# Two Mamba layers: du times B for two slots in succession, then both scans, and y's transposes ahead of B's spread

## The chip, the cores and the metric

The kernel runs on one core of a Trainium2 chip. The core has five engines that run side by side, each through its own list of instructions in order: TensorE (PE, matrix products; PEld is its weight load), VectorE (DVE), ScalarE (ACT), GpSimd (POOL) and SyncE (SP, which issues the transfers). They wait for one another through semaphores. The metric is the device time of one execution in microseconds (us): a median over several executions, and beside it one execution that was profiled.

## The reference

The network has four residual layers on an image of 4 batches, 256 channels, 64 x 64 pixels: two attention layers (L0, L1), then a Mamba layer over 512 inner channels (L2), then a Mamba layer over four groups of 64 channels with an MLP (L3). The change touches the state recurrence of L2 and L3. For each batch, each inner channel d and each of 16 states n:

```
delta = softplus(dt @ dt_proj_w + dt_proj_b)
A = -exp(A_log)
def step(h, (d_t, u_t, B_t, C_t)):
    h   = exp(d_t * A) * h + (d_t * u_t) * B_t
    y_t = sum over n of h * C_t
h0 = 0;  ys = scan(step, h0, over 4096 tokens)
y = ys + u * D
y = y * silu(z)
out = y @ out_proj_w
```

So each (channel, state) pair has a linear recurrence over the tokens, B and C are shared by all the channels of a token, and y is summed over the 16 states.

## The kernel before

**Tiles, blocks and slots.** The tokens of a batch (4096) are cut in 4 chunks of NC = 1024, and the inner channels in 4 groups of 128 (in L3, the four channel groups have 128 inner channels each). One group of one chunk is a block, with 128 channels on the partitions and 1024 tokens along the free dimension. There are 16 blocks for a batch and a layer, and each has DS = 16 slots, one for each state n. `scan_blocks` goes through the 256 slots of a batch and a layer in one loop, by hand: the order in which the calls stand is the order on each engine. It runs 8 times (two layers, four batches), so there are 2048 slots. In between lie the attention layers and the layers' beginnings and ends, which the change does not touch.

**What one slot i does, by engine.**

- `load_c` (SP, L925) brings C's row to all partitions (`cb`); three slots ahead.
- `spread` (PE, L949) makes B's row on all partitions by two products of 512 columns into a PSUM tile `pb`. The PSUM pool `psb` has two such tiles, so the tile of slot i+2 is that of slot i, and spread(i+2) waits until the scan of slot i has read it.
- In the slots named by `apart` (n = 0, 5, 10 in L2, 0, 4, 8 in L3) B comes by a transfer into `bb` instead (L931), GpSimd multiplies it with du (`product`, L935), and the decay exp(delta A) goes into the PSUM tile (`dap`, ACT, L961) in the place of B.
- In all other slots VectorE multiplies B with du in place in PSUM (L1019), and the decay is an SBUF tile `da` (ACT, L961, four buffers, three slots ahead).
- The scan (DVE, L1025) makes h of 1024 tokens. The last slot of a run is done in two halves.
- GpSimd multiplies h with C (`hc`, L1031, three buffers).
- `turn` (PE, L977) transposes hc in eight pieces of 128 columns and adds them up in a PSUM tile y over the 16 states. It is done one slot late: slot i's body turns slot i-1.
- `keep` (ACT, L966) puts the last column of h away as the next chunk's state.

**What else stands in a slot's body.** `blk["bg"]` holds steps of other work (projections, convolutions, norms and MLP of neighbouring blocks) by slot number; `end` finishes the block before (fin_ps on PE at L998 and L1002, then a product on VectorE at L991). In a body the order is: product and scan on DVE; GpSimd's product(i+2) and hc; ACT's decay(i+3) and keep; the loads; the steps of `bg` and `end`; spread(i+2); steps named n + 0.5; turn(i-1); `dap` of slot i+2. So on TensorE each body is: other work, spread of slot i+2, transposes of slot i-1.

**PSUM.** Two `pb` tiles of two banks, one y tile of two banks, and two tiles `mm` of one bank for everything else.

Of the kernel before, what the change touches and what calls it, by code (L numbers as in the profile page):

```python
# [12 lines left out]
ALU = mybir.AluOpType  # L13
# [31 lines left out]
class Net:  # L45
# [858 lines left out]

    def scan_blocks(self, blocks, loop, psum, psb, psy, apart, ends, first, last=None):
        nc = self.nc
        slots = [(blk, n) for blk in blocks for n in range(DS)]
        halves = [slice(s, s + NT) for s in range(0, NC, NT)]  # L910
        pb, da, cb, h, hc = {}, {}, {}, {}, {}
        n_slot, n_f32 = len(slots), 2


        def is_apart(i):
            return 0 < i < n_slot and slots[i][1] in apart

        def pieces(i):
            return halves if i == n_slot - 1 else [slice(0, NC)]

        def load_c(i):
            if i < len(slots):
                blk, n = slots[i]
                cb[i] = loop.tile([P, NC], F32, tag="cb", name="cb", bufs=4)
                nc.sync.dma_start(cb[i], blk["cd"][1, n].partition_broadcast(P))  # L925

        def load_b(i):
            if is_apart(i):
                blk, n = slots[i]
                pb[i] = loop.tile([P, NC], F32, tag="bb", name="bb", bufs=1)  # L930
                nc.sync.dma_start(pb[i], blk["cd"][0, n].partition_broadcast(P))  # L931

        def product(i):
            if is_apart(i):
                nc.gpsimd.tensor_tensor(pb[i], slots[i][0]["du"], pb[i], ALU.mult)  # L935

        def spread(i):
            if i < len(slots) and not is_apart(i):
                blk, n = slots[i]
                pb[i] = psb.tile([P, NC], F32, tag="pb", name="pb")  # L940
                for ss in halves:
                    if i < n_f32:
                        nc.tensor.matmul(
                            pb[i][:, ss],
                            self.ident[64:P, 64 + n : 65 + n].to_broadcast([64, P]),
                            blk["bct"][64:P, ss], start=True, stop=True,
                        )
                        continue
                    nc.tensor.matmul(  # L949
                        pb[i][:, ss], self.pick[:, n : n + 1].to_broadcast([P, P]),  # L950
                        blk["parts"][:, ss], start=True, stop=True,
                    )

        def decay(i, in_psum=False):
            if i < len(slots) and is_apart(i) == in_psum:
                blk, n = slots[i]
                if in_psum:
                    da[i] = psb.tile([P, NC], F32, tag="pb", name="dap")
                else:
                    da[i] = loop.tile([P, NC], F32, tag="da", name="da", bufs=4)  # L960
                nc.scalar.activation(da[i], blk["delta"], AF.Exp, scale=blk["a"](n))  # L961

        def keep(i):
            if i >= 0 and not slots[i][0]["last"]:
                blk, n = slots[i]
                nc.scalar.activation(blk["state"](n), h[i][:, NC - 1 : NC], AF.Copy)  # L966


        def turn(i):
            if i >= 0:  # L970
                blk, n = slots[i]
                if n == 0:
                    blk["y"] = psy.tile([P, NC], F32, tag="y", name="y")
                t = hc.pop(i)
                for j in range(NC // P):
                    ss = slice(j * P, j * P + P)
                    nc.tensor.matmul(  # L977
                        blk["y"][:, ss], t[:, ss], self.ident, is_transpose=True,
                        start=(n == 0 and ss.start % NT == 0),
                        stop=(n == DS - 1 and ss.stop % NT == 0),  # L980
                    )

        def end(blk, n):
            if n == ends[0]:
                for ss in halves:
                    nc.scalar.activation(blk["du"][:, ss], blk["y"][:, ss], AF.Copy)
            for j, (ss, first) in enumerate(zip(halves, ends[1:])):
                if n == first + 1:  # L990
                    nc.vector.tensor_tensor(  # L991
                        blk["zs"][:, ss], blk["out", j], blk["zs"][:, ss], ALU.mult
                    )
                if n == first:
                    blk["out", j] = ps = psum.tile([P, NT], F32, tag="mm", name="fin_ps")
                    for i in range(NT // P):
                        t = slice(ss.start + i * P, ss.start + i * P + P)
                        nc.tensor.matmul(  # L998
                            ps[:, i * P : (i + 1) * P], blk["du"][:, t], self.ident,
                            is_transpose=True, start=(i == 0), stop=False,  # L1000
                        )
                    nc.tensor.matmul(ps, blk["diag_d"], blk["u"][:, ss], start=False, stop=True)  # L1002

        for i in range(3):
            load_c(i)
        for i in range(4):
            load_b(i)
        for i in range(2):
            spread(i)
        for i in range(3):  # L1010
            decay(i)
            for f in first[i]:
                f()
        for i in range(2):
            decay(i, True)
            product(i)
        for i, (blk, n) in enumerate(slots):
            if not is_apart(i):
                nc.vector.tensor_tensor(pb[i], blk["du"], pb[i], ALU.mult)  # L1019
            h[i] = loop.tile([P, NC], F32, tag="h", name="h", bufs=3)  # L1020
            for ss in pieces(i):
                state = 0.0 if blk["first"] else blk["state"](n)
                if ss.start:
                    state = h[i][:, ss.start - 1 : ss.start]
                nc.vector.tensor_tensor_scan(  # L1025
                    h[i][:, ss], da[i][:, ss], pb[i][:, ss], state, ALU.mult, ALU.add
                )
            product(i + 2)
            hc[i] = loop.tile([P, NC], F32, tag="hc", name="hc", bufs=3)
            for ss in pieces(i):  # L1030
                nc.gpsimd.tensor_tensor(hc[i][:, ss], h[i][:, ss], cb[i][:, ss], ALU.mult)  # L1031
            decay(i + 3)
            keep(i - 1)
            load_c(i + 3)
            load_b(i + 4)
            if i >= DS and n != ends[0]:
                end(slots[i - DS][0], n)
            for step in blk["bg"].get(n, ()):
                step()
            if i >= DS and n == ends[0]:  # L1040
                end(slots[i - DS][0], n)
            spread(i + 2)
            for step in blk["bg"].get(n + 0.5, ()):
                step()
            turn(i - 1)
            decay(i + 2, True)
            for d in (pb, da, cb):
                del d[i]
        if last:
            last()  # L1050
        turn(n_slot - 1)
        for n in range(ends[2] + 2):
            end(blocks[-1], n)
# [168 lines left out]
    def mamba_layer(self, x, bridge, pe_dram, w_in, w_cw, w_x, w_dt, w_out, v_dram):  # L1222
        tc, nc = self.tc, self.nc
        ND = 4
        with ExitStack() as ctx:
            wp = ctx.enter_context(tc.tile_pool(name="m2_w", bufs=1, reuse_waits="tile"))
            work = ctx.enter_context(tc.tile_pool(name="m2_a", bufs=2, reuse_waits="tile"))
            loop = ctx.enter_context(tc.tile_pool(name="m2_b", bufs=2, reuse_waits="tile"))
            dram = ctx.enter_context(tc.tile_pool(name="m2_d", bufs=2, space=DRAM))
            psum = ctx.enter_context(tc.tile_pool(name="m2_p", bufs=2, space=PSUM))  # L1230
            psb = ctx.enter_context(tc.tile_pool(name="m2_q", bufs=2, space=PSUM))
            psy = ctx.enter_context(tc.tile_pool(name="m2_y", bufs=1, space=PSUM))
# [33 lines left out]
            chunks = [dict(u=[None] * ND, blocks=[]) for _ in range(n_chunk)]  # L1266
            for k in range(n_chunk):
                for d in range(ND):
# [3 lines left out]
                        first=(k == 0), last=(k == n_chunk - 1), bg={},  # L1272
# [262 lines left out]
            first = slice(0, NT), slice(NT, NC)  # L1535
# [3 lines left out]
            def center():  # L1539
# [12 lines left out]
                    )  # L1552

            self.scan_blocks(
                [blk for c in chunks for blk in c["blocks"]], loop, psum, psb, psy, (0, 5, 10),
                (1, 2, 4), (xs0[4:6], (), xs0[6:]), center,
            )
            late_square, late_sums, late_squares, finish = late_stats
# [45 lines left out]
    def grouped_mamba_layer(self, x, bridge, begun, ws_dram, outc_dram, v_dram, out_b, load):  # L1604
        tc, nc = self.tc, self.nc
        w_in, w_cw, w_x, w_dt, w_out, w_f1, w_f2 = ws_dram
        with ExitStack() as ctx:
            wp = ctx.enter_context(tc.tile_pool(name="m3_w", bufs=1, reuse_waits="tile"))
            work = ctx.enter_context(tc.tile_pool(name="m3_a", bufs=2, reuse_waits="tile"))
            loop = ctx.enter_context(tc.tile_pool(name="m3_b", bufs=2, reuse_waits="tile"))  # L1610
# [31 lines left out]
            chunks = [dict(blocks=[]) for _ in range(n_chunk)]  # L1642
# [324 lines left out]
            for i, (k, c) in enumerate(pairs):  # L1967
# [51 lines left out]
                    put(odd, (9, 11, 10, 11, 12), delta(nk, 2 * ncol))  # L2019
                    put(odd, (13, 14), [in_z(nk, ncol, s) for s in range(2)])  # L2020
            self.scan_blocks(
                [blk for c in chunks for blk in c["blocks"]], loop, psum, psb, psy, (0, 4, 8),
                (1, 2, 2), (xs0[2:4], (), xs0[4:]),
            )

# [161 lines left out]
```

## Time and profile before

| | |
|---|---|
| Median of 3 runs | 11817.76 us (11803.92 to 11832.72) |
| The profiled execution | 11811.95 us, its span 11810.1 us |
| Span of the eight runs of `scan_blocks` (windows, rounded) | 7563 us together |
| VectorE / TensorE / GpSimd / ScalarE busy in these | 7006.5 / 6128.5 / 6600.8 / 4689.8 us |
| Mean granted TensorE clock | 0.936 of full speed |

The profile gives each engine's busy time, groups of instructions (line, engine, output and inputs, shape, count, busy time, mean duration, idle time just before them and what ended it), the waits between engines and a timeline. A TensorE duration is modelled and overlaps its neighbours: two products of 0.59 us each start 0.43 us apart.

### The profile page before, as it was taken

The numbers are of one execution on the slowest core, as the hardware profiler recorded it, in microseconds if no ns is written. First come the engines' busy times: TensorE is split into PE (matmuls) and PEld (weight loads), VectorE is DVE, ScalarE is ACT, GpSimd is POOL, SyncE is SP. The second block draws the span as 40 slices with busy tenths as digits, with TensorE's granted clock in tenths as the row PEclk, the third lists the DMA queues.
The fourth block names the chain that finished last, engine by engine and source line by source line (L and its number), as shares of the span: only waits on it lengthen the run. The fifth ranks groups of instructions, "written<-read, shape, count | busy, mean of one in ns | idle before, by whom it ended". The sixth has DMA issues, their size and how long they took to land. (4 is left out here: it accounts for less than half of the span.)

```text
span 11810.1 us, 191909 instructions
## 1 busy us (share of the span) xinstructions
PE 9965.7 (84%) x70632; PEld 5738.0 (49%) x71104; DVE 9804.7 (83%) x8342; ACT 7028.2 (60%) x13152; POOL 8773.6 (74%) x6070
## 2 busy tenths in 40 slices
PE   8998887777999888777799988877779998887777
PEld 4564554444456455444455645444435564544444
DVE  6678998998767799899876779989987678998998
ACT  4565555776456555577645655557764565555776
POOL 4666886898456688789745668868975566886897
PEclk9999998998999999899999989989999999998998
DMA  3354554454335455455433545545543354554554
GB/s 97 106 141 140 172 175 143 170 183 158 94 99 144 139 172 176 144 169 183 162 88 98 144 140 172 177 143 168 182 162 90 98 143 142 172 175 143 168 175 153
DMA packets 682507, 1742.11 MB, mean 148 GB/s; under 512 B 88896, under 2 KB 194896, under 8 KB 681312
## 3 DMA queue, kind: packets, MB, share of 16 engines
q1 hardware_dynamic: 676448, 1721.41, 45.3%
q8 instruction: 563, 9.22, 0.3%
q10 hardware_dynamic: 5120, 8.39, 0.3%
q14 instruction: 376, 3.08, 0.1%
HBM read 1601.52 MB, written 94.39 MB: 144 GB/s over the span
## 5 line engine op out<-in xcount | busy, mean ns | idle before, releaser
L1031 POOL TENSOR_TENSOR hc<-h,cb 128x1024 f32<-128x1024 f32 x2056 | 4808.6, 2350 | 794.5 <-DVE h L1025 345.2
L1025 DVE TENSOR_TENSOR_SCAN h<-da,m_state,pb 128x1024 f32<-128x1024 f32 x1248 | 2920.4, 2340 | 163.0 <-DVE pb L1019 1.9
L977 PE MATMUL y<-ident,hc 128*128 128x128 f32 x16384 | 2352.7, 291 | 446.4 <-POOL hc L1031 346.1
L977 PEld LDWEIGHTS y<-ident,hc 128*128 128x128 f32 x16384 | 2051.5, 151 | 1126.1 <-POOL hc L1031 573.0
L1019 DVE TENSOR_TENSOR pb<-du,pb 128x1024 f32<-128x1024 f32 x1672 | 2025.0, 1211 | 126.4 <-PE pb L949 103.9
L961 ACT ACTIVATE da<-delta,m_v 128x1024 f32<-128x1024 f32 x1672 | 1899.2, 1141 | 135.3 <-DVE h L1025 118.4
L949 PE MATMUL pb<-m_parts,pick 128*128 128x512 bf16 x2840 | 976.1, 414 | 842.0 <-DVE h L1025 772.6
L603 POOL TENSOR_SCALAR pr<-pr,sm,zero 128x256 f32<-128x256 f32 x2048 | 1107.2, 556 | 385.5 <-DVE sm L600 381.0
L588 ACT ACTIVATE pr<-sc,mn 128x256 f32<-128x256 f32 x2048 | 954.9, 478 | 515.7 <-DVE sm L600 399.1
L949 PEld LDWEIGHTS <-pick 128*128 128x128 bf16 x3312 | 263.7, 101 | 1788.1 <-DVE h L1025 976.7
L577 DVE TENSOR_REDUCE mn<-sc 128x4 f32<-128x1024 f32 x512 | 630.1, 1232 | 542.9 <-PE sc L565 542.8
L1025 DVE TENSOR_TENSOR_SCAN h<-da,pb 128x1024 f32<-128x1024 f32 x424 | 969.5, 2287 | 55.2 <-DVE pb L1019 1.0
L935 POOL TENSOR_TENSOR bb<-du,bb 128x1024 f32<-128x1024 f32 x376 | 888.3, 2363 | 118.1 <-DMA bb<-m_cd 110.1
L1025 DVE TENSOR_TENSOR_SCAN h<-dap,m_state,bb 128x1024 f32<-128x1024 f32 x288 | 672.3, 2334 | 66.7 <-ACT dap L961 48.7
L252 PE MATMUL conv_ps<-att_y,att_wb 128*128 128x512 f32 x1536 | 682.5, 594 | 0.0
L616 PE MATMUL pt_ps<-ident,pr 128*128 128x128 f32 x4096 | 637.9, 292 | 37.8 <-POOL pr L603 16.8
L565 PE MATMUL sc<-kv,q_swap 32*64 32x128 f32 x8192 | 594.5, 283 | 26.6 <-DMA kv<-kv_dram 9.8
L961 ACT ACTIVATE dap<-delta,m_v 128x1024 f32<-128x1024 f32 x376 | 419.7, 1116 | 314.6 <-DVE h L1025 239.3
L565 PE MATMUL sc<-kv,att_y 32*64 32x128 f32 x7168 | 577.1, 282 | 28.7 <-DMA kv<-kv_dram 22.9
L616 PEld LDWEIGHTS pt_ps<-ident,pr 128*128 128x128 f32 x4096 | 459.3, 146 | 165.6 <-POOL pr L603 108.4
L290 DVE SCALAR_TENSOR_TENSOR lp<-vimg,att_v,lp 128x512 f32<-128x512 f32 x672 | 507.7, 756 | 30.4 <-DVE lp L290 0.5
L565 PEld LDWEIGHTS sc<-kv,att_y 32*64 32x64 f32 x7168 | 428.1, 136 | 161.3 <-ACT pr L588 70.5
(303 smaller groups left out, 17818.2 us busy)
## 6 DMA issues: line engine op xcount, KB each, us to landing
cb<-m_cd SPq DMA_DIRECT2D x2048, 512.0 KB, 3.9
kv<-kv_dram SPq DMA_DIRECT2D x1984, 128.0 KB, 2.8
bb<-m_cd SPq DMA_DIRECT2D x376, 512.0 KB, 5.0
kv_dram<-kst SPq DMA_DIRECT2D x128, 256.0 KB, 3.4
kv_dram<-vn SPq DMA_DIRECT2D x128, 256.0 KB, 4.2
q_swap<-att_y SPq DMA_DIRECT2D x96, 256.0 KB, 4.3
m_pe<-in_pe_dram SPq DMA_DIRECT2D x32, 512.0 KB
out_dram<-yo SPq DMA_DIRECT2D x64, 256.0 KB, 2.0
```

The costliest lines, as they stand in the source:

```text
L252: nc.tensor.matmul(ps, w[:, k, w0 + m * P : w0 + (m + 1) * P], src[:, k], start=(k == 0), stop=(k == 1),)
L565: nc.tensor.matmul(sc[h][b * 64 : b * 64 + 64, r, w, m, :], (own(sj, m) if r == b else swap[sj % 2][:, m])[rows, 2 * a + w], kv[i, w][rows ...
L588: nc.scalar.activation(t[:, g].rearrange("p j r t -> p r j t"), sc[h][:, :, g // 2, g % 2, :].rearrange("p r (j t) -> p r j t", j=2), AF.E ...
L603: nc.gpsimd.tensor_scalar(t[:, g], t[:, g], s[:, g : g + 1], self.zero, ALU.mult, ALU.add)
L616: nc.tensor.transpose(pt[h][j][:, g, :], t[:, g, j].rearrange("p r t -> p (r t)"), self.ident,)
L935: nc.gpsimd.tensor_tensor(pb[i], slots[i][0]["du"], pb[i], ALU.mult)
L949: nc.tensor.matmul(pb[i][:, ss], self.pick[:, n : n + 1].to_broadcast([P, P]), blk["parts"][:, ss], start=True, stop=True,)
L961: nc.scalar.activation(da[i], blk["delta"], AF.Exp, scale=blk["a"](n))
L977: nc.tensor.matmul(blk["y"][:, ss], t[:, ss], self.ident, is_transpose=True, start=(n == 0 and ss.start % NT == 0), stop=(n == DS - 1 and ...
L1019: nc.vector.tensor_tensor(pb[i], blk["du"], pb[i], ALU.mult)
L1025: nc.vector.tensor_tensor_scan(h[i][:, ss], da[i][:, ss], pb[i][:, ss], state, ALU.mult, ALU.add)
L1031: nc.gpsimd.tensor_tensor(hc[i][:, ss], h[i][:, ss], cb[i][:, ss], ALU.mult)
```

## The change

The loop of `scan_blocks` gets a further list of state numbers, `twos`: (2, 4, 7, 9, 12, 14) in L2, (2, 6, 10, 12, 14) in L3. Slot i is the first of two when slot i+1 has its number in that list, i is above 4 and i is not the last. In that case:

- du times B of slots i and i+1 are both issued on VectorE, and then the scan of i, what the body of i has for VectorE, and the scan of i+1;
- in the body of i, turn(i-1) stands ahead of spread(i+2) instead of behind it.

No instruction is added or removed.

```
+    def scan_blocks(self, blocks, loop, psum, psb, psy, apart, twos, ends, first, last=None):
...
+        def with_next(i):
+            return 4 < i < n_slot - 1 and slots[i + 1][1] in twos
+
+        def times_du(i):
+            if not is_apart(i):
+                nc.vector.tensor_tensor(pb[i], slots[i][0]["du"], pb[i], ALU.mult)
...
         for i, (blk, n) in enumerate(slots):
-            if not is_apart(i):
-                nc.vector.tensor_tensor(pb[i], blk["du"], pb[i], ALU.mult)
+            if not (i and with_next(i - 1)):
+                times_du(i)
+            if with_next(i):
+                times_du(i + 1)
             h[i] = loop.tile([P, NC], F32, tag="h", name="h", bufs=3)
...
+            if with_next(i):
+                turn(i - 1)
             spread(i + 2)
             for step in blk["bg"].get(n + 0.5, ()):
                 step()
-            turn(i - 1)
+            if not with_next(i):
+                turn(i - 1)
             decay(i + 2, True)
...
-                [blk for c in chunks for blk in c["blocks"]], loop, psum, psb, psy, (0, 5, 10),
+                [blk for c in chunks for blk in c["blocks"]], loop, psum, psb, psy, (0, 5, 10), (2, 4, 7, 9, 12, 14),
...
-                [blk for c in chunks for blk in c["blocks"]], loop, psum, psb, psy, (0, 4, 8),
+                [blk for c in chunks for blk in c["blocks"]], loop, psum, psb, psy, (0, 4, 8), (2, 6, 10, 12, 14),
```

More of the change, by code (lines that the diff above doesn't have):

```diff
@@ L896, in col_stats @@
         )
-    def scan_blocks(self, blocks, loop, psum, psb, psy, apart, ends, first, last=None):
+    def scan_blocks(self, blocks, loop, psum, psb, psy, apart, twos, ends, first, last=None):
         nc = self.nc
```

## The prediction

> **What bounds the kernel now.** I read first the page's groups by line, then the busy time of the eight scan stretches, then the timeline of a quiet and of a crowded piece of them. Some rows of the groups (line, engine, operation, count | busy, mean ns | idle before, releaser):
>
> ```profile
> L1031 POOL TENSOR_TENSOR hc<-h,cb 128x1024 f32<-128x1024 f32 x2056 | 4808.6, 2350 | 794.5 <-DVE h L1025 345.2
> L1025 DVE TENSOR_TENSOR_SCAN h<-da,m_state,pb 128x1024 f32<-128x1024 f32 x1248 | 2920.4, 2340 | 163.0 <-DVE pb L1019 1.9
> L1019 DVE TENSOR_TENSOR pb<-du,pb 128x1024 f32<-128x1024 f32 x1672 | 2025.0, 1211 | 126.4 <-PE pb L949 103.9
> L949 PE MATMUL pb<-m_parts,pick 128*128 128x512 bf16 x2840 | 976.1, 414 | 842.0 <-DVE h L1025 772.6
> ```
>
> VectorE hardly waits before products and scans, while TensorE's spread (L949) waits for the scan. The busy time by stretch, for the fourth stretch (L3) and the sum of all eight (us, then PE, PEld, DVE, ACT, POOL):
>
> ```profile
> 4916.00:5867.00 951.00, 729.59 (x3427) 402.87 (x3487) 873.25 (x531) 662.20 (x959) 852.33 (x388) 0.91 0.52 175
> sum 7563.00, PE 6128.47 PEld 3476.03 DVE 7006.50 ACT 4689.80 POOL 6600.81; mean PE 766.06 PEld 434.50 DVE 875.81 ACT 586.23 POOL 825.10
> ```
>
> VectorE is busy for 7006 of 7563 us; it is the bound here, with GpSimd (6601) and TensorE (6128) not far below. Now VectorE's rows in a quiet piece:
>
> ```profile
> 10735.66 1.21 DVE L1019 TENSOR_TENSOR pb<-du,pb 128x1024 f32<-128x1024 f32 x1
> ...
> 10737.00 2.35 DVE L1025 TENSOR_TENSOR_SCAN h<-da,m_state,pb 128x1024 f32<-128x1024 f32 x1
> ...
> 10739.27 1.21 DVE L1019 TENSOR_TENSOR pb<-du,pb 128x1024 f32<-128x1024 f32 x1
> ...
> 10740.61 2.35 DVE L1025 TENSOR_TENSOR_SCAN h<-da,m_state,pb 128x1024 f32<-128x1024 f32 x1
> ```
>
> From product to its scan: 10735.66 + 1.21 = 10736.87, start 10737.00, a gap of 0.13. From scan to the next product: 10739.35, start 10739.27, 0.08 *before* the end. Counted over the timeline, the median step from one of the 1672 products to its scan is 0.133 and from a scan to the next product -0.084. An instruction that needs the one just ahead of it pays 0.217 us more than one that doesn't.
>
> **The change, part by part.**
>
> *Gain.* In a pair the order is product, product, scan, scan: no instruction needs the one just ahead of it, so two steps of 0.217 go, 0.434 us. Pairs: L2 has 6 in each of 64 blocks less 2 in each of the 4 first ones, 376; L3 5 x 64 - 4 = 316. 692 x 0.434 = 300 us. The nearest rows for product after product are the 316 steps from another VectorE instruction to a product (median -0.084); bounds are 0 (every step as 0.13) and 300; I take 300.
>
> The Trainium skill (VectorE: DVE Perf Modes, The DRAIN you can't avoid) states that the next VectorE instruction doesn't start before the pipe is empty and that fewer semaphores save nothing. By that rule the reordering would regain nothing, and the sum below would end near 12,276; the step of -0.08 above speaks against it.
>
> *Cost: the second product comes too early for its B.* Spread(i+1) can't begin before scan i-1 has freed the tile. Before, a product and a scan (3.61 us) lay between product i and product i+1; now it is the product alone, 1.13 (1.21 - 0.08). What spread was late by up to 2.48 us was hidden and now stalls VectorE, and with it both scans. With nothing in TensorE's way a spread starts 0.05 after the scan and takes 0.59, and the product follows 0.04 later: 0.68, inside 1.05. But other work stands ahead of it. A crowded piece, from the scan of an apart slot (n = 5) on:
>
> ```profile
> 4300.68 2.32 DVE L1025 TENSOR_TENSOR_SCAN h<-dap,m_state,bb 128x1024 f32<-128x1024 f32 x1
> ...
> 4302.92 0.66 DVE L991 TENSOR_TENSOR m_zs<-fin_ps,m_zs 128x512 f32<-128x512 f32 x1
> ...
> 4303.50 1.22 DVE L1019 TENSOR_TENSOR pb<-du,pb 128x1024 f32<-128x1024 f32 x1
> ...
> 4303.64 1.98 PE L1314 MATMUL u_ps<-m_xn,m_wxi 128*128 128x512 f32 x4 [0.68 <-DVE m_zs L991]
> ...
> 4305.46 0.59 PE L949 MATMUL pb<-m_parts,pick 128*128 128x512 bf16 x2
> ...
> 4307.11 1.21 DVE L1019 TENSOR_TENSOR pb<-du,pb 128x1024 f32<-128x1024 f32 x1
> ```
>
> Scan 5 ends at 4303.00, VectorE does L991 (whose PSUM tile u_ps needs next), product 6 starts at 4303.50; u_ps starts at 4303.64 and spread 7 behind it ends at 4306.05. Product 7 could now start at 4304.63, but not before 4306.09: a stall of 1.46 where before there was none (4307.11).
>
> I counted this for all 692 second products in the timeline of before: (end of spread + 0.04) - (start of first product + 1.13), not below 0 and not above 2.48 (beyond that the old order stalled too). 219 have no stall, 410 more than the 0.434 that the pair gains. Sum 642 us: 433 at the 376 pairs behind an apart slot (L2 196, L3 237), 209 at the other 316.
>
> Not all is paid. A stall lets TensorE catch up, so the next spread is less late; turn(i-1) ahead of spread(i+2) runs while TensorE would wait for the scan, and takes some 0.9 us out of the way of the next spread; and later waits of VectorE (some 340 us of steps over 0.2 us lie in the eight stretches) may take up a stall. I walked two blocks slot by slot with their rows: the L2 block around the piece above counts 7.3 us of stalls and keeps 5.6 (at 7 the whole stall, at 9 none because of it, at 14 1.0 where the count says 0); an L3 block (the sixth of the fourth stretch) counts 6.3 and keeps 4.6, mostly because the stall at 10 is won back where VectorE waited for delta (L1156) before. That is 0.75; many blocks being less crowded, I take 0.70: 449 us. Bounds 0 and 642.
>
> *Turn moved.* Eight transposes (0.13 apart, 1.04) now go ahead of the spread in 692 bodies. They need hc of slot i-1, whose scan ended a whole pair's products and a scan (4.5 us) before scan i; GpSimd takes 2.35 for it. While GpSimd is on time they cost nothing; where it is behind, spread(i+2) waits with them, and the first product of the next pair after it (its cover is the second scan, 2.27). No cost taken of its own; it lies within the 30% that I left out or not.
>
> *Other engines.* In L2 two scans now go straight into an apart slot (3, 4, 5 and 8, 9, 10), so `dap` has 2.25 instead of 3.5 us after scan i-2. In before, `dap` of n = 5 and 10 ended past 2.25 by 114 us in all and past 3.5 by 49, so between 0 and 65 us come on top; scan i-2 itself comes a product later against ScalarE's list, so I take 15. GpSimd gets its hc in bursts: three in 7.05 us plus `product` 2.36, and needs h buffers back 6.7 us after the scan; 0 while it isn't behind. Transfers keep their places on SP: 0.
>
> *Sum*, against the profiled execution of 11,812 us: -300 + 449 + 15 = +164, 11,976; the runs' median lies 6 us above that execution, so about 11,980, rounded down to 11,975.
>
> **Rivals.**
>
> *TensorE catches up (faster).* If the lateness of spread is mostly carried over from earlier bodies, one stall cures the next ones: then the stalls behind pairs vanish (209) and half of those behind apart slots (216): 216 - 300 = -84, 11,730; with no stall at all 11,518. For: TensorE is busy 6128 of 7563 us, modelled, so it has room. Against: in the piece above its wait is for VectorE's own L991, which comes only after the apart scan. It wins where the stalls sum below 300, 47% of the count.
>
> *The whole bill.* Stalls are paid in full and `dap` too: 642 + 65 - 300 = +407, 12,225. For: GpSimd at 852 of 951 us in L3 can hold the moved transposes back. Against: the two walks.
>
> *No gap regained.* The second product now carries a wait for VectorE's own semaphore as well (for the scan before the pair); if it keeps the step at 0.13, 449 + 15 = +464, 12,282. Against: that scan ended a product earlier.
>
> *The sides cancel*: within 24 us of before.
>
> **How the numbers follow.** Forecast 0.56 (its own range 11,845 to 12,100, stalls of 52 to 92% of the count), catching up 0.23, whole bill 0.12, no gap regained 0.04, cancel 0.05. From 11,720 to 12,140 it leaves out about half of the faster case and the upper part of the dear ones. About 0.2% (24 us) is what a measurement of this kernel tells from no change. Faster 0.23, same 0.05, slower 0.72.
>
> **What would show it.** Right: scans right behind each other at -0.08 and no 0.13 gap in pairs; idle before L1019 released by PE pb L949 up from 104 us to some 500; the gap's total down by 300. The largest stalls at the second products n = 7, 12 (L2), 2, 10 (L3). Wrong: idle before L1019 under 300 us, or a product-product step above 0.1, or new idle before the scans released by `dap` or GpSimd.

## The result, and the profile after

The changed kernel takes 12,337.7 us (median of 4 runs, 12,330.8 to 12,342.4) against 11,812.9 for the kernel before on the same chip: a ratio of 1.0444, 95% interval 1.0431 to 1.0457. It is slower, as forecast, but by 525 us instead of 164; the time lies above the stated range (12,140).

The groups by line of the changed kernel (line numbers have moved: scan 1034, product 923, spread 956, transposes 984, hc 1040):

```profile
L1040 POOL TENSOR_TENSOR hc<-h,cb 128x1024 f32<-128x1024 f32 x2056 | 4797.7, 2347 | 1460.3 <-DVE h L1034 556.8
L984 PE MATMUL y<-ident,hc 128*128 128x128 f32 x16384 | 2435.6, 298 | 855.0 <-POOL hc L1040 682.9
...
L1034 DVE TENSOR_TENSOR_SCAN h<-da,m_state,pb 128x1024 f32<-128x1024 f32 x1248 | 2872.6, 2329 | 26.2 <-POOL yo L1863 0.5
L923 DVE TENSOR_TENSOR pb<-du,pb 128x1024 f32<-128x1024 f32 x1672 | 2015.1, 1218 | 969.9 <-PE pb L956 967.3
```

Two idle times tell the story. Ahead of the scans it falls from 163.0 us to 26.2: the gap between a product and its scan is gone where there is a pair. Ahead of the products it rises from 126.4 to 969.9, and 967.3 of that ends with the spread of B on TensorE.

Busy time in the fourth scan stretch and the sum of all eight (us, then PE, PEld, DVE, ACT, POOL):

```profile
5125.00:6149.00 1024.00, 774.77 (x3484) 418.18 (x3485) 862.75 (x532) 666.16 (x959) 851.14 (x387) 0.88 0.48 163
...
sum 8082.00, PE 6449.06 PEld 3576.82 DVE 6910.83 ACT 4718.72 POOL 6592.17; mean PE 806.13 PEld 447.10 DVE 863.85 ACT 589.84 POOL 824.02
```

The stretches grew from 7563 to 8082 us, so practically the whole loss lies in them. VectorE has the same instructions as before and is busy for 6911 of 8082 us instead of 7006 of 7563. TensorE's busy time rose by 320 us with the same products; its granted clock fell (0.88 against 0.91 in this stretch, 0.917 against 0.936 over the run). Some 45 us of the 320 are a matter of records: the trace of before shows 2840 of the spread's 3312 products (at 472 slots the second of the two is missing), and the changed kernel's trace shows all:

```profile
L956 PE MATMUL pb<-m_parts,pick 128*128 128x512 bf16 x3312 | 1122.0, 425 | 583.5 <-DVE h L1034 516.9
```

The 45 is an estimate, with the missing products put where the recorded ones lie.

The piece of the prediction's crowded timeline, in the changed kernel:

```profile
4482.95 2.32 DVE L1034 TENSOR_TENSOR_SCAN h<-dap,m_state,bb 128x1024 f32<-128x1024 f32 x1
...
4485.19 0.66 DVE L998 TENSOR_TENSOR m_zs<-fin_ps,m_zs 128x512 f32<-128x512 f32 x1
...
4485.78 1.22 DVE L923 TENSOR_TENSOR pb<-du,pb 128x1024 f32<-128x1024 f32 x1
...
4485.91 1.98 PE L1326 MATMUL u_ps<-m_xn,m_wxi 128*128 128x512 f32 x4 [0.47 <-DVE m_zs L998]
4487.73 0.59 PE L956 MATMUL pb<-m_parts,pick 128*128 128x512 bf16 x2
...
4488.37 1.23 DVE L923 TENSOR_TENSOR pb<-du,pb 128x1024 f32<-128x1024 f32 x1 [1.37 <-PE pb L956]
...
4489.51 4.58 DVE L1034 TENSOR_TENSOR_SCAN h<-da,m_state,pb 128x1024 f32<-128x1024 f32 x2
```

It is as foretold here: product 7 waits 1.37 us (forecast 1.46) for a spread behind u_ps, which itself waited for VectorE. Then both scans follow without a gap.

For the whole run I added up VectorE's idle steps over 0.2 us ahead of each product and each apart scan:

| us, all eight stretches | before | after |
|---|---|---|
| second products behind an apart slot (376) | 75 | 610 |
| second products behind a pair (316) | 9 | 215 |
| product 3 of L3 (not in a pair) | 4 | 94 |
| all others | 137 | 176 |
| sum | 225 | 1096 |

That is 871 us more, and 300 us come back from the gaps: 571, of which some 50 are taken up where VectorE waited before for other things (its waits for delta alone fall from 103.9 to 56.5 us). The stretches' growth is 519.

### The profile page after: what moved, and what is told of

Same layout as the page of the kernel before. It is cut to its first block, busy times and chain, and to the rows that moved or that the text cites. A ratio compares the mean times of both kernels' runs of the same rounds, so it can differ in the third digit from the quotient of the medians.

```text
span 12336.1 us, 193673 instructions
## 1 busy us (share of the span) xinstructions
PE 10293.4 (83%) x71104; PEld 5836.4 (47%) x71104; DVE 9706.3 (79%) x8342; ACT 7052.4 (57%) x13152; POOL 8761.6 (71%) x6070
## 5 line engine op out<-in xcount | busy, mean ns | idle before, releaser
L984 PE MATMUL y<-ident,hc 128*128 128x128 f32 x16384 | 2435.6, 298 | 855.0 <-POOL hc L1040 682.9
L984 PEld LDWEIGHTS y<-ident,hc 128*128 128x128 f32 x16384 | 2081.2, 154 | 1773.2 <-POOL hc L1040 1254.5
L1034 DVE TENSOR_TENSOR_SCAN h<-da,m_state,pb 128x1024 f32<-128x1024 f32 x1248 | 2872.6, 2329 | 26.2 <-POOL yo L1863 0.5
L923 DVE TENSOR_TENSOR pb<-du,pb 128x1024 f32<-128x1024 f32 x1672 | 2015.1, 1218 | 969.9 <-PE pb L956 967.3
L956 PE MATMUL pb<-m_parts,pick 128*128 128x512 bf16 x3312 | 1122.0, 425 | 583.5 <-DVE h L1034 516.9
```

Source lines behind the costliest of these rows:

```text
L923: nc.vector.tensor_tensor(pb[i], slots[i][0]["du"], pb[i], ALU.mult)
L956: nc.tensor.matmul(pb[i][:, ss], self.pick[:, n : n + 1].to_broadcast([P, P]), blk["parts"][:, ss], start=True, stop=True,)
L984: nc.tensor.matmul(blk["y"][:, ss], t[:, ss], self.ident, is_transpose=True, start=(n == 0 and ss.start % NT == 0), stop=(n == DS - 1 and ...
L1034: nc.vector.tensor_tensor_scan(h[i][:, ss], da[i][:, ss], pb[i][:, ss], state, ALU.mult, ALU.add)
```

## The experiments

Each ran beside the kernel before; the ratio is to that. "Stalls" is the sum of the table above (225 in before).

| run | time, us | ratio, 95% interval | stalls |
|---|---|---|---|
| the change | 12,337.7 | 1.0444 (1.0431 to 1.0457) | 1096 |
| e1 pairs only | 12,316.7 | 1.0436 (1.0419 to 1.0454) | 1067 |
| e2 transposes only | 11,943.8 | 1.0116 (1.0099 to 1.0133) | 370 |
| e3 state 0's transposes behind | 12,289.8 | 1.0412 (1.0395 to 1.0430) | 1018 |
| e4 pairs, early spread | 11,861.1 | 1.0053 (1.0036 to 1.0070) | 488 |
| e5 early spread, no pairs | 11,917.7 | 1.0089 (1.0072 to 1.0106) | 242 |
| e6 e4 behind apart slots only | 11,873.9 | 1.0060 (1.0043 to 1.0077) | 368 |
| e7 e1, half the transposes | 12,230.9 | 1.0359 (1.0340 to 1.0378) | 959 |
| e8 before, half the transposes | 11,719.2 | 0.9922 (0.9905 to 0.9938) | 194 |
| e9 e7, half of hc | 11,966.7 | 1.0129 (1.0112 to 1.0145) | 740 |
| e10 e8, half of hc | 11,624.0 | 0.9840 (0.9823 to 0.9856) | 139 |
| e11 picked pairs | 11,848.2 | 1.0030 (1.0017 to 1.0044) | 346 |
| e12 pairs behind apart slots only | 12,222.4 | 1.0344 (1.0327 to 1.0361) | 825 |
| e13 clean pairs | 11,770.1 | 0.9966 (0.9952 to 0.9979) | 213 |

**e1 and e2: the two parts alone.** e1 takes the moved transposes back; e2 keeps them and undoes the pairs.

```
e1:  -            if with_next(i):
     -                turn(i - 1)
                  spread(i + 2)
     ...
     -            if not with_next(i):
     -                turn(i - 1)
     +            turn(i - 1)
e2:  -            if not (i and with_next(i - 1)):
     -                times_du(i)
     -            if with_next(i):
     -                times_du(i + 1)
     +            times_du(i)
```

> The two products and two scans in a row as in the change, but y's transposes stay behind B's spread. Theory A (the moved transposes hold the spread back on TensorE, waiting for hc and for the copy of y into du): the waits of y for du (135 us) and the extra waits for hc (683 against 346 us) go, and what is left is the stalls counted in the trace of before, 449 to 642 us, less 300: 11,960 to 12,155. Theory B (the stalls come from the pairs alone, the moved transposes help or are neutral): not under 12,300.

> Product and scan alternate as before; only y's transposes go ahead of the spread in the same slots. Theory A: TensorE's waits for du and hc appear as in the changed kernel, but the 3.6 us between one product and the next hide part of them: 11,840 to 12,000. Theory B: no loss, 11,780 to 11,830.

Theory A, my first one after the result, falls for e1: the pairs alone cost 510 us. By themselves the moved transposes cost 137 us, inside A's range, but on top of the pairs no more than the intervals leave open (1.0444 and 1.0436 overlap). So the pairs carry the loss. In e1 VectorE's wait for the spread and TensorE's wait for the scan rise together (before: 103.9 and 772.6 us):

```profile
PE pb L956 <- DVE h L1034: 1079.3, 666, 3.7
DVE pb L923 <- PE pb L956: 918.0, 484, 6.9
```

Each waits more for the other. That is not a TensorE that has too much to do. In e1's trace 349 second products stall for more than 0.434 us and have a spread to come for the slot behind their pair; in 259 of these places that spread starts within 0.1 us of the end of the pair's first scan, and TensorE stood idle ahead of it for 1.69 us on average. So in three places of four the stall is handed on to the next spread, and TensorE can't use it to catch up.

**e3: where a new y begins.** The transposes of state 0 are the first to write y, whose only PSUM tile ScalarE copies into du in the body of state 1.

```
-            if with_next(i):
+            if with_next(i) and n != 1:
                 turn(i - 1)
...
-            if not with_next(i):
+            if not with_next(i) or n == 1:
                 turn(i - 1)
```

> The change, but where the first of two is state 1 the transposes (those of state 0, which begin a new y) stay behind the spread. Theory A with the copy of y into du as the main wait: PE's wait of y for du falls from 135 us to under 10, the stalls of L3's product 3 (94 us) and part of those of L2's 3 and 4 go: 12,150 to 12,260. If the waits for hc carry it, or under theory B: 12,310 to 12,345.

Between both ranges: 483 us over the kernel before, where the change is 525 over it. The mechanism is there; in the changed kernel's timeline (fourth stretch, third block):

```profile
5262.20 1.06 ACT L995 ACTIVATE du<-y 128x512 f32<-128x512 f32 x2
...
5263.36 1.94 PE L984 MATMUL y<-ident,hc 128*128 128x128 f32 x8 [5.86 <-ACT du L995]
...
5265.10 1.06 PE L956 MATMUL pb<-m_parts,pick 128*128 128x512 bf16 x2
...
5266.19 1.23 DVE L923 TENSOR_TENSOR pb<-du,pb 128x1024 f32<-128x1024 f32 x1 [2.80 <-PE pb L956]
```

The transposes wait 5.86 us for the copy, the spread stands behind them, and product 3 waits 2.80 us. In e3 the stall at product 3 of L3 falls from 94 to 4 us; some of it comes back at other products (L2's 4: 57 to 98).

**e4, e5 and e6: the spread ahead of the other work.**

```
e4 (on e1):  +            if with_next(i + 1):
             +                spread(i + 2)
                          ...        (end and bg steps)
             -            spread(i + 2)
             +            if not with_next(i + 1):
             +                spread(i + 2)
e5 (on e4):  times_du(i) alone, no pairs
e6 (on e4):  twos (2, 7, 12) in L2, (2, 6, 10) in L3
```

> Pairs, transposes behind the spread, and in the bodies that spread a second product's B this spread stands ahead of the body's other work. If the second product's stall is TensorE's other work ahead of the spread (0.68 us without it, against a cover of 1.05), these stalls go and the 300 us of the gap remain less what TensorE loses by waiting for the scan: 11,520 to 11,700. If TensorE's loss by waiting outweighs it: 11,820 to 12,100.

> Product and scan alternate as before; the spread of the same slots as in e4 stands ahead of the body's other work. It measures what e4's order costs TensorE by itself. If the pairs are worth their 300 us once the second product's B is in time, e4 (11,861) is this kernel less some 200 to 300: 12,050 to 12,150. If the order costs nothing by itself and the pairs' gain is given back elsewhere: 11,790 to 11,870.

> e4 with pairs and early spread only behind the apart slots (376 pairs, states 1-2, 6-7, 11-12 in L2 and 1-2, 5-6, 9-10 in L3), none of which runs straight into an apart slot. The gap is worth 163 us. If what e4 gives back is at the apart slots that follow a pair (dap 137 and bb 74 us of waits against 75 and 26 before): 11,660 to 11,760. If it is the early spread itself that costs, also here: 11,800 to 11,900.

In e4 the idle time before the products falls from e1's 919.1 us to 282.7:

```profile
L923 DVE TENSOR_TENSOR pb<-du,pb 128x1024 f32<-128x1024 f32 x1672 | 1997.2, 1217 | 282.7 <-PE pb L956 272.8
```

The second products stall 130 us instead of e1's 902. So it is work ahead of the spread in TensorE's list that makes these stalls. But the order costs by itself (e5: +104 us over the kernel before; VectorE's idle steps ahead of the scans are 79 us longer), and with B in time the pairs win only some 50 of their 300 us (e4: +55): stalls rise from 242 to 488, 130 us of that at second products and 80 at apart scans. The lower granted clock is not what makes the loss: it is 0.928 in e1 and in e5, and they lose 510 and 104 us. e6 has fewer stalls and fewer pairs and ends where e4 does: 11,874, in the range for "the early spread itself".

**e7 to e10: is it TensorE's transposes, or GpSimd's products?** e7 and e8 do four of eight transposes, e9 and e10 also half of hc.

```
e7, e8:   -                for j in range(NC // P):
          +                for j in range(4 * (n % 2), 4 * (n % 2) + 4):
e9, e10:  -            for ss in pieces(i):
          -                nc.gpsimd.tensor_tensor(hc[i][:, ss], h[i][:, ss], cb[i][:, ss], ALU.mult)
          +            ss = halves[n % 2]
          +            nc.gpsimd.tensor_tensor(hc[i][:, ss], h[i][:, ss], cb[i][:, ss], ALU.mult)
```

> e1 with only four of each slot's eight transposes (even states the first 512 columns of y, odd states the others), so half the terms of y are left out and TensorE has 0.43 to 0.5 us less in each slot. If the second products' stalls are TensorE's other work ahead of the spread, the pairs' loss over the same kernel without pairs (e8) falls from 510 us to under 300. If the stalls come from waits (for VectorE, ScalarE, GpSimd) it stays over 400.

> The kernel before with four of each slot's eight transposes, half the terms of y left out as in e7. VectorE bounds, TensorE's lateness is hidden by the 3.6 us between products: 11,700 to 11,800, little faster than before.

> e7 with GpSimd multiplying only the half of h that is transposed (even states the first 512 columns, odd states the others), so half of h times C is left out and GpSimd has some 1.15 us less in each slot. If the second products' stalls come from transposes that wait for hc on TensorE ahead of the next spread, the pairs' loss against the same kernel without pairs (e10) falls from e7's 512 us to under 300. If it is other work ahead of the spread, it stays over 400.

> e8 with half of h times C left out as in e9. VectorE bounds and GpSimd's lateness is mostly hidden: 11,600 to 11,720.

The pairs cost 510 us with all the transposes and 512 with half of them (12,230.9 - 11,719.2). Less TensorE work does not lessen the loss as a whole, though the granted clock also fell in both (0.874 and 0.888), which takes part of the relief back. The second products do stall less: 686 us more than without pairs, where it was 819 in e1; what takes this up elsewhere stays open. The two kernels without pairs, e8 and e10, land in their ranges. With half of hc the loss is 343 us (11,966.7 - 11,624.0): between the two ranges, so a third of it hangs on GpSimd's work. TensorE's waits for hc with the pairs, in e7 and then in e9:

```profile
PE y L984 <- POOL hc L1040: 487.6, 400, 4.3
...
PE y L984 <- POOL hc L1040: 57.5, 71, 3.3
```

The stalls that the pairs add are 164 us fewer with half of hc (601 instead of 765). Of that, 107 us lie at the second products behind apart slots, where transposes that waited for hc stood in front of the spread, and 38 at the apart scans, which wait for GpSimd's own `product`. The transposes' waits are thus a part of the third, and how large a part was not tried by itself.

**e11, e12 and e13: which pairs.**

```
e11, e13 (on e1):  -            return 4 < i < n_slot - 1 and slots[i + 1][1] in twos
                   +            return 4 < i < n_slot - 1 and (slots[i + 1][1], (i + 1) // DS) in twos
                   (twos is here a list of (state, block))
e12 (on the change): twos (2, 7, 12) in L2, (2, 6, 10) in L3
```

> e1's order, but only the 58 places (block and state; 232 pairs over four batches) where the trace of before counts a spread at most 0.15 us too late for a second product. The gap is worth 232 x 0.434 = 101 us. If the count of lateness in the trace of before foretells the stalls when no other pairs are there: 11,690 to 11,740. If pairs make lateness of their own (the first scan comes a product later and with it the next spread, as at state 14 in L2, where e1 stalls 0.6 to 3.6 us though the count says none): 11,780 to 11,900.

> The change with pairs only behind the apart slots (376 of 692: states 2, 7, 12 in L2 and 2, 6, 10 in L3). By the count of before 433 of the 642 us of stalls lie there, in the trace of the changed kernel 610 of 862; the gap gives 163 back. If the stalls stay where they are without the other pairs: 12,230 to 12,330. If they are made by the pairs that went before in the block: 11,950 to 12,150.

> e1's order at only the 29 places (116 pairs over four batches) that in e11 had no stall of their own and made none in the next three slots. The gap is worth 116 x 0.434 = 50 us. If what VectorE saves reaches the end of the run where no spread is late: 11,755 to 11,785 for a kernel before of 11,814. If it is given back at other engines all the same: 11,800 to 11,830.

e12 lands 8 us under its first range: without the other pairs, the second products behind apart slots still stall 558 us (610 in the change). So most of these stalls are made on the spot. e11 is the telling miss of the count: 232 pairs where the old trace showed at most 0.15 us of lateness, and yet 34 us slower. A part is the trace's: at 40 of these pairs it lacks the spread's second product, which ends 0.22 to 0.43 us after the first, and so could not show the whole lateness. But they have only 24 of the 70 us that the 232 second products stall now. Before, in L2's fifth block, from the scan of state 11 on:

```profile
4209.11 2.35 DVE L1025 TENSOR_TENSOR_SCAN h<-da,m_state,pb 128x1024 f32<-128x1024 f32 x1
...
4211.52 0.60 PE L949 MATMUL pb<-m_parts,pick 128*128 128x512 bf16 x2 [0.85 <-DVE h L1025]
...
4212.83 1.02 PE L1390 MATMUL out_ps<-x,ident 128*128 128x512 f32 x2
...
4215.41 0.59 PE L949 MATMUL pb<-m_parts,pick 128*128 128x512 bf16 x2
...
4215.56 1.22 DVE L1019 TENSOR_TENSOR pb<-du,pb 128x1024 f32<-128x1024 f32 x1
```

and in e11 the same place, states 11 and 12 being a pair, and 13 and 14 too:

```profile
4219.62 2.35 DVE L923 TENSOR_TENSOR pb<-du,pb 128x1024 f32<-128x1024 f32 x2
...
4221.88 4.58 DVE L1034 TENSOR_TENSOR_SCAN h<-da,m_state,pb 128x1024 f32<-128x1024 f32 x2
...
4224.28 0.61 PE L956 MATMUL pb<-m_parts,pick 128*128 128x512 bf16 x2 [1.77 <-DVE h L1034]
...
4225.60 1.02 PE L1399 MATMUL out_ps<-x,ident 128*128 128x512 f32 x2
...
4226.96 1.22 DVE L923 TENSOR_TENSOR pb<-du,pb 128x1024 f32<-128x1024 f32 x1
4228.17 0.59 PE L956 MATMUL pb<-m_parts,pick 128*128 128x512 bf16 x2
...
4228.80 1.23 DVE L923 TENSOR_TENSOR pb<-du,pb 128x1024 f32<-128x1024 f32 x1 [0.62 <-PE pb L956]
```

The list that TensorE goes through from scan 11 to spread 14 (spread 13, transposes, out_ps) takes the same time: spread 14 starts 6.30 us after the start of scan 11 before (4215.41 - 4209.11) and 6.29 after it in e11 (4228.17 - 4221.88). But product 12 now stands ahead of scan 11 instead of behind it. TensorE waits longer for that scan (1.77 us instead of 0.85 at spread 13), and VectorE is at product 13 already 5.08 us after the start of scan 11 (4226.96) instead of 6.45 (4215.56). So product 14 comes too early and stalls 0.62 us at a place where the old trace had shown room. Here a pair makes the next pair's lateness.

e13 keeps the 116 pairs that stalled neither themselves nor a neighbour, and is faster than the kernel before: 38 us by the medians, 0.9966 (0.9952 to 0.9979), of 50 worked out. There the gap does reach the end of the run. Its groups:

```profile
L1034 DVE TENSOR_TENSOR_SCAN h<-da,m_state,pb 128x1024 f32<-128x1024 f32 x1248 | 2910.2, 2338 | 138.6 <-DVE pb L923 2.4
...
L923 DVE TENSOR_TENSOR pb<-du,pb 128x1024 f32<-128x1024 f32 x1672 | 2017.5, 1212 | 114.0 <-PE pb L956 82.5
```

Idle time before the scans falls by 24 us (163.0 before), and before the products it doesn't rise (126.4 before).

## Why the prediction was wrong

**The gap (-300): right.** In the changed kernel the median step from a pair's second product to the scan behind it is -0.091 us (0.133 from a product to its scan before), from scan to scan -0.084, and from product to product -0.09 in the third that doesn't stall (243 of 692). e13 shows that such a gap is worth its price where nothing else is late. The rival that no gap would be regained is out: the next instruction starts 0.08 us before the end of the one ahead if it doesn't need it, and 0.13 us after it if it does. For these rows the sentence of the Trainium skill that the prediction draws on (VectorE: DVE Perf Modes, The DRAIN you can't avoid) does not hold; the same section goes on to say that a next instruction that is not held starts earlier, which the prediction left out.

**The stalls (+449): the step that failed.** The count was 642, and I took 0.70 of it because "a stall lets TensorE catch up". Measured, the second products stall 742 us more than before (826 less 84): 206 behind pairs, where I counted 209, and 535 behind apart slots, where I counted 433. In sum nothing was forgiven. The reason is the order on VectorE itself: the stalled second product stands ahead of the first scan, so the stall delays that scan, the spread that waits for its tile, and all that stands behind this spread on TensorE. e1's two rising waits and its spreads that start with the delayed scan show that, and e11's timeline shows the same for a scan that a product has put back. e7 speaks against the amount of TensorE's work as the main reason. My walks by hand let TensorE run on through a stall. That 206 is so near the 209 counted is luck: without the moved transposes (e1) it is 284. This term alone is 293 us of the 361 that the sum was short.

**Why more behind apart slots than counted** is settled in part: e9 against e7 shows that GpSimd's lateness has a share in the loss, and e12 that the other pairs have little. The count itself was short as well: at 148 of the 692 places (72 of the 376 behind apart slots) the trace of before lacks the spread's second product, so the spread's end was taken too early by 0.22 to 0.43 us. With that added the whole count would be some 21 to 42 us higher, 11 to 20 of it behind apart slots (an estimate). How the rest of the missing 102 us divides was not tried.

**The transposes (0): wrong.** I weighed their wait for hc and missed that those of state 0 begin a new y and wait for ScalarE's copy. The transposes' row before, and then PE's waits of the changed kernel:

```profile
L977 PE MATMUL y<-ident,hc 128*128 128x128 f32 x16384 | 2352.7, 291 | 446.4 <-POOL hc L1031 346.1
...
PE y L984 <- POOL hc L1040: 682.9, 493, 4.0
PE pb L956 <- DVE h L1034: 516.9, 511, 3.7
PE y L984 <- ACT du L995: 135.1, 52, 5.9
```

Waits for hc were 346.1 us before, for the copy 3.8. Alone the move costs 137 us (e2). Together with the pairs it costs little more than they do: it brings 90 us at product 3 of L3, and behind pairs the second products stall 215 us instead of e1's 293.

**`dap` (+15): too small to see.** Stalls at L2's apart scans 5 and 10 go from 39 to 41 us.

**The rivals.** "TensorE catches up" is out. The whole bill, 12,225, was the nearest, and still 110 us too low, since stalls behind apart slots and the wait for the copy go beyond it.

**Slips in the working that change little.** The forecast's own range, 11,845 to 12,100, is 52 to 92% of the count less the gap, without the 15 of `dap`. The eight transposes start 0.109 us apart, not 0.13 (that is their 1.04 us over eight). And a spread takes 0.59 us at the full clock, but 1.06 in the piece shown with e3, where the granted clock was 0.50: then even a spread with nothing in its way has its product follow after 0.05 + 1.06 + 0.04 = 1.15 us, later than the cover of 1.05.

## What to carry to other kernels

When two engines hand one buffer back and forth, moving an instruction that consumes ahead of one that releases tightens the circle: count the cover between release and next use in both directions, and let a stall delay everything that waits for the stalled instruction. Lateness hidden in the old order is no upper bound of the new stalls: here they came to 742 us against 642 counted. Take such a reordering place by place: with 116 of the 692 pairs, chosen by their stalls in e11's trace, it made the kernel 0.3% faster, and with all of them 4.4% slower. Before moving work ahead of a critical instruction, look for the one iteration that begins a new buffer.

## What the hardware showed that I had not expected

TensorE's granted clock is lower where work is taken from it or waits are put into it: 0.936 before, 0.917 in the changed kernel, 0.888 and 0.874 with half the transposes left out (e8, e7). It does not go by the idle time alone: e1 leaves TensorE idle for longer than the change does (busy for 10,159 of 12,320 us against 10,293 of 12,336) at a higher clock, 0.928. One pause can be followed in the piece shown with e3: the granted clock falls to 0.50 at 5262.65 us, 0.7 us before the end of the 5.86 us in which the transposes wait for the copy, and is back at 1.00 at 5266.06; in between eight transposes take 1.94 us and the spread 1.06, where the prediction has 1.04 and 0.59. That agrees in direction with the Trainium skill (TensorE: Matmul & The Clock Gate, Part 1), which states that the clock is halved after an idle window and released after a busy one. So less work or a further wait on TensorE can make the rest of its work slower: the mean transpose takes 291 ns before, 298 in the changed kernel, 312 in e8 and 317 in e7.
